# One PSUM pool of eight banks, rows transposed a tile ahead, and tiles dealt out in three runs, in a decoder layer with routed experts

## The chip, the cores and the metric

The kernel runs on one core of a Trainium2 chip. A core has five engines with instruction streams of their own: TensorE (matrix products and transposes, written to PSUM), VectorE, ScalarE, GpSimd (POOL in the profile) and SyncE (SP), which here only starts transfers. PSUM has eight banks of 128 partitions by 512 fp32 values. The metric is the device time of one execution in microseconds; of several executions the median is given.

## The reference

One decoder layer on 64 sequences of 128 positions with 256 features, all in fp32. Cut to what matters:

```
def attn(x):                                # a selective scan
    x_inner, z = split(layernorm(x) @ W_in)                 # 256 -> 2 x 512
    x_conv = silu(conv(x_inner, conv_w) + conv_b)           # 4 taps per channel
    Bmat, Cmat, delta = split(x_conv @ W_x)                 # 16, 16, 1
    h[t] = exp(delta[t] * A) * h[t-1] + delta[t] * Bmat[t] * x_conv[t]
    y = Cmat . h + x_conv * D_skip
    return (y * silu(z)) @ W_out + x

def xattn(q, c):                            # retention
    return ((xpos(q @ Wq) @ xpos(c @ Wk).T) * decay_mask) @ (c @ Wv)

def ffn(x):                                 # 8 experts, 2 per row, and a shared one
    shared = (silu(x @ shared_gate.T) * (x @ shared_up.T)) @ shared_down.T
    scores, indices = top_k(sigmoid(x @ router_w.T + routing_bias), 2)
    scores = scores / sum(scores)
    return shared + sum_k scores[k] * expert[indices[k]](x) # silu(gate) * up, then down; inner size 512

x = layernorm(x + attn(x)); x = layernorm(x + xattn(x, ctx)); x = layernorm(x + ffn(x))
```

## The kernel before

**Chains.** The 64 sequences go through in 16 groups (NG) of 4, 512 rows each. For each group `first_half` does layer norm, W_in, the convolution and the scan, which is written as products of decay matrices instead of a loop over positions. Its steps appear in the profile by their tiles: `w_in_s`, `xc`, `w_x_s`, `bcs`, `d` and `after_in` (sums of delta over positions), `cj` and `bj` (C and B with their decays, made on VectorE at L745), `mt` and `xd` (the decay matrix times the rows). `second_half` does W_out (`w_out_s`, `sz`), the retention, a layer norm, and then `route`: logits (`rw`, `logit`), the rank of each expert per row, the count of rows per expert so far (`sel`, `upto`, `pre`), and a scatter of each row to the place of its two experts in a DRAM buffer `xs`, by indirect DMAs on POOL. The comparisons that make ranks and the order mask `mk` (L968) are VectorE's, and the product `sel,upto` waits for them.

**The shared expert.** `shared` makes gate, up and down products for one group's 512 rows: per block of 128 inner features a gate and an up product, each filling a bank `psg`, `psu`; silu on ScalarE, the product with `up` on VectorE (`hc`, L1016), and at the end the down products. For nine groups this runs early, beside the next chains; for groups 7 to 13 (LATE) it runs at the end of the kernel.

**Routed tiles.** The rows in `xs` are worked off in 78 tiles of one expert each, in five batches (BATCHES: 9, 16, 16 and 16 tiles of 256 rows, after groups 4, 8, 12 and 16, and 21 of 128 rows at the end). `tile_list` makes each batch's table `what` on VectorE: tile number n (the constant `number`, an iota) is compared with the running sum `cum` of tiles per expert, which gives the tile's expert, its first row in `xs`, and a flag whether that expert differs from the one three tiles before. Three buffers of 1.5 MB (NW = 3) hold an expert's weights; tile i uses buffer i % 3, and its load is left out when the flag is zero. `fetch` starts both transfers on SP's queue: rows (L1142), then weights (L1148). `one_tile` calls `hidden` (the rows transposed to `rows_T`, copied out by ScalarE at L1166, then gate and up, silu at L1182, the product at L1183) and after it `down` of the tile before, whose rows are scaled by the routing weight (L1196) and scattered by POOL (L1197). Only when `down` has been called does `room` allow the load three tiles on. At the end `combine` gathers each row's two products, adds them, and does the last layer norm.

**PSUM.** Two pools share the eight banks: `pm` with five serves the chains, the transposes of tiles and their `down`; `gu` with three serves the shared expert and the gate and up products of tiles.

**What sets the order.** Each stage is a generator. `abreast` lets four of them run side by side (first halves, second halves, shared experts, tiles) and always continues the one that is least advanced in its due place, which `placed` gives it. The clock of this plan is `work`, to which every matmul and transpose adds an estimate; a `yield` with a number asks not to be continued for so long. `there` notes when a tile's rows and weights are to be expected. The order of emission then gives priorities, and the framework's scheduler lays out each engine's stream by priority, by readiness, and by the slots of the pools.

## Time and profile before

| | |
|---|---|
| three executions, median (lowest, highest) | 2053.07 us (2049.54, 2053.74) |
| profiled execution, its own time | 2046.0 us |
| its span, first to last instruction | 2044.3 us |
| mean granted TensorE clock in it | 0.984 |
| TensorE matmuls busy | 1894.9 us, 9252 instructions |
| VectorE, ScalarE, POOL busy | 988.5, 743.1, 462.0 us |
| read from HBM, written | 207.33 MB, 58.60 MB |
| SP's weight issues | 78 of 1536 KB |

A line of the timeline reads: start and length of a run of like instructions, engine, source line, operation, out<-in by the program's names, shape, how many; in square brackets the idle time before it and the instruction that ended it. Every fp32 product is recorded as two instructions. Line L543 is the helper that issues nearly all products, so that its groups are told apart by tile names. In the waits, a row names the engine and tile that waited, then the one that released it, then total, number and longest. A window's row has its two ends, its length, busy time and count of five engines, then the granted clock, the share of DMA time and GB/s.

### The profile page before, as it was taken

The page shows a single profiled execution, that of the slowest core. Times are in us where ns is not written, and L with a number is a line of the kernel's source. Part 1 is how long each engine was busy: PE and PEld are TensorE (multiplying, and loading weights), DVE is VectorE, ACT ScalarE, POOL GpSimd, SP SyncE. Part 2 cuts the span into 40 slices and gives each one's busy share as a digit, 9 for nine tenths or more (in the row PEclk, how much of TensorE's full clock was granted, in tenths as well). Part 3 has the DMA queues.
Part 4 walks back from the last instruction along what each step waited for, and adds up shares of the span by engine and source line. Part 5 has one row for each costly group of instructions (what it writes and reads, how often), then busy time and mean ns, then how long its engine had stood idle before and what let it go on. Part 6 is the DMA issues. An engine that isn't in the chain of part 4 may idle for free. (4 is left out here: it accounts for less than half of the span.)

```text
span 2044.3 us, 26096 instructions
## 1 busy us (share of the span) xinstructions
PE 1894.9 (93%) x9252; PEld 1396.5 (68%) x9252; DVE 988.5 (48%) x2398; ACT 743.1 (36%) x1239; POOL 462.0 (23%) x697
## 2 busy tenths in 40 slices
PE   4989998999999999999999999998998999999996
PEld 2655666686767676777777676767676888886553
DVE  3667676565555564555555555554431111012574
ACT  3355344344343534353434252534121222221332
POOL 3030221221212122323223121222123222221110
PEclk9899999999999999999999999999999999999998
DMA  4011121422313234333333442433224555862772
GB/s 146 26 54 44 53 64 39 165 90 75 124 44 109 59 135 150 111 126 124 129 121 100 150 140 80 134 116 116 104 80 166 183 184 195 305 218 97 256 268 84
DMA packets 100629, 253.60 MB, mean 124 GB/s; under 512 B 22824, under 2 KB 60328, under 8 KB 91528
## 3 DMA queue, kind: packets, MB, share of 16 engines
q1 hardware_dynamic: 77368, 196.56, 29.1%
q0 software_dynamic: 17616, 52.46, 7.4%
q10 hardware_dynamic: 5504, 2.81, 0.5%
q8 instruction: 75, 1.23, 0.2%
q14 instruction: 66, 0.54, 0.1%
HBM read 207.33 MB, written 58.60 MB: 130 GB/s over the span
## 5 line engine op out<-in xcount | busy, mean ns | idle before, releaser
L543 PE MATMUL gu<-rows_T,routed_w 128*128 128x256 f32 (+1 forms) x2496 | 511.2, 358 | 40.3 <-ACT rows_T L1166 14.8
L543 PEld LDWEIGHTS gu<-rows_T,routed_w 128*128 128x128 f32 x2496 | 421.5, 193 | 115.8 <-issue 34.1
L1183 DVE TENSOR_TENSOR hid<-hid,gu 128x512 f32<-128x512 f32 x135 | 92.3, 686 | 389.4 <-PE gu L543 370.5
L543 PE MATMUL pm<-routed_w,hid 128*128 128x256 f32 x1080 | 258.4, 383 | 9.9 <-DVE hid L1183 9.9
L543 PE MATMUL pm<-xnT,w_in_s 128*128 128x512 f32 x512 | 243.4, 600 | 3.2 <-ACT xnT L580 3.1
L543 PE MATMUL gu<-x2T,shared_w 128*128 128x512 f32 x512 | 230.5, 596 | 3.5 <-DVE hc L1016 2.6
L543 PEld LDWEIGHTS pm<-routed_w,hid 128*128 128x128 f32 x1080 | 198.6, 190 | 51.3 <-DVE hid L1183 14.7
L1197 POOL DMA_INDIRECT ys<-rows_out,to x135 | 138.4, 1026 | 325.5 <-ACT rows_out L1196 252.4
L562 POOL TENSOR_TENSOR rstd<-var,mhalf 128x4 f32<-128x4 f32 x64 | 68.2, 1066 | 508.7 <-DVE mv L558 282.7
L628 DVE SCALAR_TENSOR_TENSOR xc<-pm,cw,xc 128x508 f32<-128x508 f32 (+2 forms) x192 | 141.2, 740 | 77.9 <-ACT xc L623 74.3
L543 PEld LDWEIGHTS gu<-x2T,shared_w 128*128 128x128 f32 x512 | 94.6, 190 | 111.5 <-issue 99.6
L1182 ACT ACTIVATE hid<-gu 128x512 f32<-128x512 f32 x135 | 80.5, 596 | 237.6 <-PE gu L543 217.4
L543 PEld LDWEIGHTS pm<-xnT,w_in_s 128*128 128x128 f32 x512 | 95.6, 193 | 87.2 <-issue 74.1
L567 ACT ACTIVATE x<-x,shift,rstd 128x256 f32<-128x256 f32 x132 | 72.6, 591 | 183.1 <-DVE shift L564 183.1
L543 PE MATMUL pm<-w_out_s,sz 128*128 128x256 f32 x512 | 122.0, 391 | 9.3 <-DVE sz L784 8.3
L1196 ACT ACTIVATE rows_out<-pm,wt 128x256 f32<-128x256 f32 x135 | 57.7, 469 | 199.0 <-PE pm L543 148.5
L543 PE MATMUL gu<-shared_w,hc 128*128 128x256 f32 x512 | 116.7, 382 | 7.3 <-DVE hc L1016 7.3
L543 PEld LDWEIGHTS pm<-w_out_s,sz 128*128 128x128 f32 x512 | 98.5, 195 | 32.9 <-DVE sz L784 14.1
L543 PEld LDWEIGHTS gu<-shared_w,hc 128*128 128x128 f32 x512 | 95.4, 190 | 26.9 <-DVE hc L1016 11.1
L992 POOL DMA_INDIRECT xs<-x,index x64 | 66.9, 1045 | 138.3 <-issue 75.4
L781 DVE SCALAR_TENSOR_TENSOR xc<-xc,dsk,pm 128x512 f32<-128x512 f32 x64 | 47.2, 744 | 84.5 <-PE pm L543 56.3
L623 ACT ACTIVATE xc<-pm,cb,cw 128x512 f32<-128x512 f32 x64 | 49.7, 777 | 105.1 <-PE pm L543 105.1
(233 smaller groups left out, 2465.6 us busy)
## 6 DMA issues: line engine op xcount, KB each, us to landing
routed_w<-in_ffn_dram SPq DMA_DIRECT2D x78, 1536.0 KB
picked<-ys SPq DMA_DIRECT2D x16, 1024.0 KB
rows_in<-xs SPq DMA_DIRECT2D x57, 258.0 KB
cT<-in_ctxT_dram POOLq DMA_DIRECT2D x16, 512.0 KB
cq<-chunks SPq DMA_DIRECT2D x16, 512.0 KB
x_rows<-x SPq DMA_DIRECT2D x16, 512.0 KB
xt<-in_x_dram POOLq DMA_DIRECT2D x10, 512.0 KB
xt<-x_rows SPq DMA_DIRECT2D x10, 512.0 KB
```

The source lines that it names most:

```text
L543: nc.tensor.matmul(out, lhsT=lhsT, rhs=rhs, **how)
L562: nc.gpsimd.tensor_tensor(rstd, var, mhalf, ALU.pow)
L567: nc.scalar.activation(dst[:, b, :], src[:, b, :], AF.Identity, bias=shift[:, b : b + 1], scale=rstd[:, b : b + 1])
L623: nc.scalar.activation(xcf[:, c, :], ps, AF.Identity, bias=cb[:, c : c + 1], scale=cw[:, c, TAPS - 1 : TAPS],)
L628: nc.vector.scalar_tensor_tensor(xc[:, c, :, s:], ps3[:, :, : L - s], cw[:, c, TAPS - 1 - s : TAPS - s], xc[:, c, :, s:], ALU.mult, ALU.add,)
L781: nc.vector.scalar_tensor_tensor(y, xcf[:, c, :], dsk[:, c : c + 1], ps.rearrange("p b l -> p (b l)"), ALU.mult, ALU.add)
L992: s = nc.gpsimd.indirect_dma_start(out=xs, in_=rows[k][:, b, :], in_offset=None, out_offset=bass.IndirectOffsetOnAxis(ap=index[:, b, k : k ...
L1182: nc.scalar.activation(hc, psg, AF.Silu)
L1183: nc.vector.tensor_tensor(hc, hc, psu, ALU.mult)
L1196: nc.scalar.activation(y[:, j, :], ps[:, j, :], AF.Copy, scale=wt[:, j : j + 1])
L1197: s = nc.gpsimd.indirect_dma_start(out=ys, in_=y[:, j, :], in_offset=None, out_offset=bass.IndirectOffsetOnAxis(ap=to[:, j : j + 1], axis=0),)
```

## The change

There is one pool, `pm`, with eight banks; all its tiles share one tag, so any of them can take any bank. The transposes of a tile's rows, their copy to `rows_T`, and the small copies `to` and `wt` move to a function `rows_turned`. `hidden(i)` calls it for the next tile, between the two gate/up blocks of a 256-row tile or after the only one of a 128-row tile, if that tile's rows are due by `work`; otherwise the next `hidden` begins with it. And the constant `number` becomes a table for each size of batch, in which positions 0, 3, 6... hold the first third of the tile numbers, 1, 4, 7... the second and 2, 5, 8... the last, so that each weight buffer works through one run of the list.

```diff
-    pm = ctx.enter_context(tc.tile_pool(name="pm", bufs=5, space=bass.MemoryType.PSUM))
-    gu = ctx.enter_context(tc.tile_pool(name="gu", bufs=3, space=bass.MemoryType.PSUM))
+    pm = ctx.enter_context(tc.tile_pool(name="pm", bufs=8, space=bass.MemoryType.PSUM))
...
-            psg = gu.tile([P, T], F32, name="gu")
+            psg = pm.tile([P, T], F32, name="gu", tag="pm")
...
-            ge, number[:, 0:n].unsqueeze(2).to_broadcast([1, n, NE]),
+            ge, numbers[n].unsqueeze(2).to_broadcast([1, n, NE]),
...
-        nc.vector.scalar_tensor_tensor(row, number[:, 0:n], float(size), row, ALU.mult, ALU.add)
+        nc.vector.scalar_tensor_tensor(row, numbers[n], float(size), row, ALU.mult, ALU.add)
...
-    def hidden(i, t):
+    def rows_turned(i, t):
         _, size = shape(i)
-        w = weights[i % NW]
-        wg = w[:, 0:SZ].rearrange("p (k i) -> p k i", k=KD)
-        wu = w[:, SZ : 2 * SZ].rearrange("p (k i) -> p k i", k=KD)
         ps = pm.tile([P, KD, size], F32, name="pm")
...
-        yield 1.2
+        turned_rows.append((tT, to, wt))
+
+    turned_rows = []
+
+    def hidden(i):
+        _, size = shape(i)
+        w = weights[i % NW]
+        wg = w[:, 0:SZ].rearrange("p (k i) -> p k i", k=KD)
+        wu = w[:, SZ : 2 * SZ].rearrange("p (k i) -> p k i", k=KD)
+        if not turned_rows:
+            rows_turned(i, ahead.pop(0))
+            yield 1.2
+        tT, to, wt = turned_rows.pop()
         hid = []
         each = T // size
         for c0 in range(0, CF, each):
-            psg = gu.tile([P, each, size], F32, name="gu")
-            psu = gu.tile([P, each, size], F32, name="gu")
+            psg = pm.tile([P, each, size], F32, name="gu", tag="pm")
+            psu = pm.tile([P, each, size], F32, name="gu", tag="pm")
...
             hid += [hc[:, c, :] for c in range(each)]
+            if ahead and not turned_rows and there[i + 1] - 8.0 <= work[0]:
+                rows_turned(i + 1, ahead.pop(0))
         return hid, to, wt
...
-        made = yield from hidden(i, ahead.pop(0))
+        made = yield from hidden(i)
...
-    number = const.tile([1, MOST], F32, name="number")
-    nc.gpsimd.iota(number, pattern=[[1, MOST]], base=0, channel_multiplier=0,
-                   allow_small_or_imprecise_dtypes=True)
+    numbers = {}
+    for n in sorted({n for _, _, n, _ in BATCHES}):
+        t = const.tile([1, -(-n // NW), NW], F32, name=f"number{n}")
+        nc.gpsimd.iota(t, pattern=[[1, -(-n // NW)], [n // NW, NW]], base=0, channel_multiplier=0,
+                       allow_small_or_imprecise_dtypes=True)
+        for s in range(1, NW):
+            if n % NW:
+                nc.vector.tensor_scalar(t[:, :, s], t[:, :, s], float(min(s, n % NW)), None, ALU.add)
+        numbers[n] = t.rearrange("p k s -> p (k s)")[:, 0:n]
```

More of the change, by code (lines that the diff above doesn't have):

```diff
@@ L1009, in shared @@
         for c in range(CF):
-            psg = gu.tile([P, T], F32, name="gu")
+            psg = pm.tile([P, T], F32, name="gu", tag="pm")
             project(psg, wg, c * P, x2T)
-            psu = gu.tile([P, T], F32, name="gu")
+            psu = pm.tile([P, T], F32, name="gu", tag="pm")
             project(psu, wu, c * P, x2T)
@@ L1019, in shared @@
         for j in range(GB // 2):
-            ps = gu.tile([P, 2, D], F32, name="gu")
+            ps = pm.tile([P, 2, D], F32, name="gu", tag="pm")
             for i in range(2):
```

## The prediction

> **What bounds the kernel.** I read the page's busy shares first, then TensorE's waits, then its timeline around each wait. Columns of the waits: total us, times, longest.

> ```profile
> span 2044.3 us, 26096 instructions
> ...
> PE 1894.9 (93%) x9252; PEld 1396.5 (68%) x9252; DVE 988.5 (48%) x2398; ACT 743.1 (36%) x1239; POOL 462.0 (23%) x697
> ```

> TensorE is busy 1894.9 us of 2044.3 and no other engine passes 48%. So a microsecond counts only where it opens or closes a hole in TensorE's row, or slows its clock. The holes, about 135 us in all, are named by the waits:

> ```profile
> PE gu L543 <- ACT rows_T L1166: 14.8, 16, 3.2
> PE gu L543 <- DMA routed_w<-in_ffn_dram: 13.3, 6, 4.2
> PE gu L543 <- ACT hid L1182: 11.5, 7, 1.8
> ...
> PE pm L543 <- DVE mk L968: 10.4, 8, 4.0
> PE pm L543 <- DVE cj L745: 10.1, 5, 3.7
> ...
> PE pm L543 <- DVE hid L1183: 9.9, 17, 0.6
> ```

> Rows 1, 3 and 6 are what the change aims at: tiles that wait for their own turned rows, for a `gu` bank that ScalarE's silu has yet to empty, and for their own `hid`. Row 2 is all that 78 conditional loads cost today. The `mk` and `cj` rows are the chain's latency on VectorE (ranks, decay matrix), and matter because of what covers them:

> ```profile
> 187.29 4.56 PE L543 MATMUL gu<-x2T,shared_w 128*128 128x512 f32 x10
> 193.11 1.13 PE L543 MATMUL pm<-cj,bj 128*128 128x128 f32 x8 [1.25 <-DVE cj L745]
> ...
> 194.51 4.46 PE L543 MATMUL gu<-x2T,shared_w 128*128 128x512 f32 x10
> 199.53 0.38 PE L543 MATMUL pm<-sel,upto 128*128 128x32 f32 x2 [0.56 <-DVE mk L968]
> ...
> 201.45 3.59 PE L543 MATMUL pm<-mt,xd 128*128 128x128 f32 x30
> ```

> Two blocks of ten shared-expert matmuls, 9 us, lie inside the latencies of `cj` and `sel`, so holes of 1.25 and 0.56 are left. One group on, a single pair is left for the second place, and the hole is 3.97:

> ```profile
> 338.39 1.02 PE L543 MATMUL gu<-x2T,shared_w 128*128 128x512 f32 x2
> 343.38 0.61 PE L543 MATMUL pm<-sel,upto 128*128 128x32 f32 x2 [3.97 <-DVE mk L968]
> ...
> 347.11 4.67 PE L543 MATMUL pm<-mt,xd 128*128 128x128 f32 x30
> ```

> The same 30 matmuls took 3.59 and 4.67 us. The granted clock (the figure before the last two) says why:

> ```profile
> 343.60:347.00 3.40, 3.40 (x18) 3.40 (x18) 1.35 (x5) 2.53 (x5) 0.00 (x0) 0.50 0.00 0
> ...
> 1236.80:1240.20 3.40, 2.45 (x6) 1.99 (x7) 0.86 (x2) 0.00 (x0) 0.00 (x0) 0.50 0.00 0
> ```

> **The change, part by part.** The profiled run is 2046.0, its span 2044.3; the runs' median is 2053.07. I sum differences against 2046.0 and add them to the median.

> *(a) One pool of eight banks: where it frees.* With 5 and 3 banks a tile's second gate/up block needs a fourth `gu` bank and waits for a silu. In each of the six or seven groups between 795 and 1500 us the timeline shows the same holes: 0.76 (`rows_T`), 1.83 (`hid` L1182), 0.65 (`rows_T`), 0.44 (`x`). Three of the 16 `rows_T` waits lie elsewhere (0.74, 2.44, 0.1), so 11.6 of it goes here with part (b), the 11.5 of `hid` L1182 goes, and 2.3 of `x`. In the changed instruction order the router transpose (`logit`) stands without cover; by its neighbours (transpose out, copy, back) about 0.95, seven times. 11.6 + 11.5 + 2.3 - 6.6 = 18.8, **gain 19** (bounds 12 to 27). Between 370 and 750 us 3 of `rows_T` goes, and with the 2.44 hole its clock dip (10 us at 0.83, so 1.7): **gain 4.7**. From 1500 to 1600 one `hc` wait of 1.6 goes: **1.6**. In the last stretch (late shared experts) some bank waits go: **gain 3** (0 to 6).

> *(a) where it takes cover away.* The scheduler gives the slots of one pool out in program order. Before, shared-expert blocks had their own slots and were taken whenever the chain's next step wasn't ready, which is how 2, 5 and 5 matmul pairs got into each early group's latencies. In the changed order none stands between `rw` and `sel` in groups 1 to 4; they stand among w_out and w_in matmuls, where TensorE had nothing to wait for. The same work, hence no change of busy time, but the holes open: by the fourth group's bare `sel`, 3.97 plus the 0.6 to 1.0 it still had as cover, 4.6; at `cj` the fill was 4.6 and the hole 1.25, but two activation-table loads of 1.28 that the silu put into ScalarE's part of that chain leave too, so 2.2 to 2.8; `logit`, `d1` and `pre` 2.2 together. That is 9.5 a group where 2.2 were: 7.3 each for three groups, 4 for the fourth (half bare already), less the 2.2 that group 1 waits for `xnT` today: **loss 23** (10 to 30). At the eighth group, 720 to 745 us, 12 tile matmuls and 8 shared ones leave the same place, and `cj` and `sel` follow bare: **loss 8** (3 to 10).

> *The clock.* After the 3.97 hole TensorE ran at 0.50 for about 6.8 us: the transposes of `xc` and `mt,xd` took 2.8 to 3.0 us longer than the same ones at 199 to 205. Three more holes of 4.6, each behind one of 2.5, are as deep: 3 x 3.0 = 9.0, the fourth 0.7 more, the eighth group 2.0 (a dip of 1.7 stands nearby already). **Loss 11.7.** [...] holes of 1.39 and 1.28 within 4 us were followed by 0.50 at 1236.8[...]. Against it, the same pair at 1340 and 3.15 at 1416 brought nothing. I take the row of the like hole, 3.0[...].

> *(b) Rows turned a tile ahead.* The 2 or 4 transposes, the copy to `rows_T` (L1166) and POOL's copies `to` and `wt` move from the head of a tile into the one before; none is added. Their rows must land one tile earlier; they are loaded up to three tiles ahead, so I cost it at nothing; if SP is late, TensorE stands behind the transposes for up to a load, about 2 us. POOL's two small copies now precede the scatter of the tile before; POOL is at 23%. `down` of a tile now follows the gate/up of the next, so the late 128-row tiles lose this hole:

> ```profile
> 1779.08 3.73 PE L543 MATMUL gu<-rows_T,routed_w 128*128 128x128 f32 x32
> 1782.65 0.38 PE L547 MATMUL pm<-ident,rows_in 128*128 128x128 f32 x2
> 1783.66 1.99 PE L543 MATMUL pm<-routed_w,hid 128*128 128x256 f32 x8 [0.63 <-DVE hid L1183]
> 1785.49 3.73 PE L543 MATMUL gu<-rows_T,routed_w 128*128 128x128 f32 x32
> ```

> 17 x 0.63 and a bank wait of 1.04 at 1760: **gain 11.7**. But the buffer comes free one tile later. From the end of `down` to the gate/up that needs the next load there are then 3.57 + 0.3 + 1.83 = 5.7 us. An undisturbed load takes 6.35 to 6.45 from issue to its last packet at 1805 to 1824, and 0.2 passes before the issue: 0.85 late. Behind it wait that gate/up and everything on TensorE. Six or seven executed loads: **loss 6** (3 to 15). [...] The trace's own loads decide. With 256-row tiles the window is 10.8, and a load is hidden.

> *(c) Tiles dealt in three runs.* With the reference's routing the load flag is set in 69 of 78 tiles before and in 39 after; 30 x 1.57 MB = 47 MB less of 207. All but six loads are hidden, so this alone is worth little: at 1549, 1582 and 1597 (4.24, 2.33, 2.86) the first three loads of a batch remain, behind SP's zero-fill transfers: nothing either way (0 to -3). In the late tiles 12 of 21 are left out, which is why only six or seven stall above. Two more iotas on POOL stand ahead of the first groups' half-width transposes: **loss 0.5**.

> **Sum.** Gains 19 + 4.7 + 1.6 + 3 + 11.7 = 40.0; losses 23 + 8 + 11.7 + 6 + 0.5 = 49.2. Net +9.2: span 2053.5, run 2055.2, median 2053.07 + 9.2 = **2062**.

> **Rivals.**
> 1. *Faster, 2037.* The early latencies shrink by more than I think when the shared silu leaves ScalarE and its product VectorE: each table load is 1.28, each `hc` product 0.69. If the chain ends 4 us sooner in each of four groups and the eighth, [...]the clock holds: losses 10 + 3 + 4 + 6 + 0.5 = 23.5 against 40, 2053 - 16.5. It decides once early holes, eighth group and clock together cost under 33. For it: the tables in the chain. Against: VectorE runs from 193 to 200 with no hole wider than 0.1, and the `hc` products are 0.7 of it before `sel`.
> 2. *Slower, 2083.* The holes come as forecast, and the late loads follow one another: stall 2 instead of 0.85 (+8), the gain between 795 and 1500 only 12 (+7), early holes at their upper end (+6). For it: 0.89 DMA share in that stretch before. Against: fewer loads share the engines now.
> 3. *No change, 2054.* All moved holes come back in kind[...]. The loads left out don't show, hidden before as after.

> **Numbers.** Forecast 0.52 (own range 2054 to 2073), faster 0.23, slower by more 0.13, no change 0.12. Repeats of this kernel differ by up to 0.2%, 4.1 us, so that is about what can be told from no change. The forecast's lower end gives part of its chance to "same": faster 0.24, same 0.16, slower 0.60. Range: 2038 takes in all but the deepest of the faster case, 2080 most of the slower.

> **What will show it.** Right: in groups 1 to 3, `sel` behind `mk` with 4 us or more and a slice of clock at 0.5 behind each; `rows_T` and `hid` L1182 gone from the waits, `hid` L1183 too; `routed_w` waits of about 0.9 in the late tiles; about 160 MB read. Wrong: `sel` holes under 2 in groups 1 to 3, a new cover there, or late stalls of 2 us or none.

## The result

The changed kernel takes 2062.14 us (median of six runs, 2058.88 to 2067.45) against 2053.4 for the kernel before on the same chip (2048.97 to 2056.0): 1.0049 times, 95% interval 1.0031 to 1.0066. It is slower by about 8.7 us; 9 were forecast. Lines of the changed kernel's page, and the line on transfers of the kernel before:

```profile
span 2057.2 us, 26112 instructions
...
PE 1896.3 (92%) x9252; PEld 1412.8 (69%) x9252; DVE 993.6 (48%) x2400; ACT 742.9 (36%) x1236; POOL 460.9 (22%) x699
...
DMA packets 96307, 206.39 MB, mean 100 GB/s; under 512 B 22344, under 2 KB 59848, under 8 KB 91048
```

```profile
DMA packets 100629, 253.60 MB, mean 124 GB/s; under 512 B 22824, under 2 KB 60328, under 8 KB 91528
```

TensorE's busy time rose by 1.4 us only, the span of the profiled execution by 12.9. That is more than the 8.7 of the medians: the profiled execution of before took 2046.0 us, less than any of the six just named, so a few us of the comparisons by trace below may not be the change's. The transfers fell from 253.60 to 206.39 MB, the 47 MB that were worked out. (The page's HBM line still says 207.33 MB read: it doesn't tell the loads that are left out.) The mean granted clock fell from 0.984 to 0.967. The largest of TensorE's waits, changed kernel (total us, times, longest):

```profile
PE pm L542 <- DVE cj L744: 27.6, 6, 6.3
PE pm L542 <- DVE mk L967: 26.2, 11, 4.6
PE gu L542 <- DMA routed_w<-in_ffn_dram: 21.0, 8, 5.0
```

The rows of before that the change aimed at (`rows_T` 14.8, `hid` L1182 11.5, own `hid` 9.9) are gone. In their place `cj` went from 10.1 to 27.6, `mk` from 10.4 to 26.2, the weights from 13.3 to 21.0. Group 3 in the timeline:

```profile
275.55 1.08 PE L542 MATMUL pm<-middle,dlb 128*32 128x128 f32 x32
282.72 2.05 PE L542 MATMUL pm<-cj,bj 128*128 128x128 f32 x8 [6.09 <-DVE cj L744]
...
288.78 0.60 PE L542 MATMUL pm<-sel,upto 128*128 128x32 f32 x2 [3.16 <-DVE mk L967]
...
292.11 4.90 PE L542 MATMUL pm<-mt,xd 128*128 128x128 f32 x32
```

There is no shared-expert block between these steps any more. And the clock in the same place, by windows (length, busy time of PE, PEld, DVE, ACT and POOL; last three columns: granted clock, DMA share, GB/s):

```profile
279.40:282.80 3.40, 0.08 (x1) 0.11 (x1) 1.93 (x5) 0.00 (x0) 0.00 (x0) 0.72 0.03 9
282.80:286.20 3.40, 2.82 (x12) 2.42 (x12) 3.40 (x6) 0.54 (x1) 0.00 (x0) 0.50 0.00 0
```

The product `sel,upto` starts once per group, so its sixteen starts cut both traces into like stretches ("5th sel" is its start in the fifth group). Difference to the kernel before, us, with the forecast's sum for the same stretch:

| stretch | forecast | measured | worked out from the starts |
|---|---|---|---|
| start to 5th sel | +33.2 | +35.3 | 463.96 - 428.64 |
| 5th to 7th | -4.7 | -3.3 | 192.26 - 195.52 |
| 7th to 8th | +10.0 | +7.4 | 101.56 - 94.12 |
| 8th to 16th | -19.0 | -25.3 | 777.23 - 802.55 |
| 16th to end | -10.3 | -1.3 | 522.2 - 523.5 |
| span | +9.2 | +12.9 | 2057.2 - 2044.3 |

So the early loss was sized well, the middle gained more than I said, and the stretch with the late tiles gained nearly nothing. That the sum came out so close is in part luck, since these two misses cancel.

### The profile page after: what moved, and what is told of

The parts are those of the page before. It is cut to its first block, busy times and chain, and to the rows that moved or that the text cites. A ratio compares the mean times of both kernels' runs of the same rounds, so it can differ in the third digit from the quotient of the medians.

```text
span 2057.2 us, 26112 instructions
## 1 busy us (share of the span) xinstructions
PE 1896.3 (92%) x9252; PEld 1412.8 (69%) x9252; DVE 993.6 (48%) x2400; ACT 742.9 (36%) x1236; POOL 460.9 (22%) x699
## 2 busy tenths in 40 slices
DMA packets 96307, 206.39 MB, mean 100 GB/s; under 512 B 22344, under 2 KB 59848, under 8 KB 91048
## 3 DMA queue, kind: packets, MB, share of 16 engines
HBM read 207.33 MB, written 58.60 MB: 129 GB/s over the span
## 4 chain that ended last, share of the span: by engine, by line
PE 67%; DVE 9%; DMA 8%; issue 8%; ACT 3%; POOL 2%; SPq 0%; another core or an unknown queue 0%; DVEq 0%; POOLq 0%; ACTq 0%
PE pm L542 36%; PE gu L542 27%; PE pm L546 4%; DMA cq<-chunks 3%; DMA routed_w<-in_ffn_dram 2%; DMA x_rows<-x 1%; POOL rstd L561 1%; DVE gq L756 1%; DVE eq L752 1%; DVE eq L751 1%; DVE st L556 1%; DMA picked<-ys 1%; POOL ys L1207 1%; DVE xc L780 1%; ACT L692 0%
## 5 line engine op out<-in xcount | busy, mean ns | idle before, releaser
L542 PE MATMUL gu<-rows_T,routed_w 128*128 128x256 f32 (+1 forms) x2496 | 504.1, 355 | 21.1 <-DMA routed_w<-in_ffn_dram 21.0
L542 PEld LDWEIGHTS gu<-shared_w,hc 128*128 128x128 f32 x512 | 96.8, 192 | 30.5 <-DVE hc L1015 12.1
L1014 ACT ACTIVATE hc<-gu 128x512 f32<-128x512 f32 x64 | 37.8, 591 | 132.0 <-PE gu L542 120.0
```

Source lines behind the costliest of these rows:

```text
L542: nc.tensor.matmul(out, lhsT=lhsT, rhs=rhs, **how)
L1014: nc.scalar.activation(hc, psg, AF.Silu)
```

## The experiments

All ratios are to the kernel before, measured on the same chip in the same set; the sets ran on different chips, so kernels of two sets are compared by their ratios only. The ratios are those on record for a whole set; the quotient of two medians given below can differ from them by up to 0.2%. The stretches of all kernels, as in the table above (one profiled execution each, us against the one profile of before, so small differences mean little; the 5th to 7th sel is left out):

| kernel | to 5th | 7th to 8th | 8th to 16th | 16th to end | ratio (95% interval) |
|---|---|---|---|---|---|
| changed kernel | +35.3 | +7.4 | -25.3 | -1.3 | 1.0049 (1.0031 to 1.0066) |
| pool_only | +39.9 | +1.1 | +3.2 | +23.7 | 1.0391 (1.0357 to 1.0425) |
| deal_only | +0.7 | 0.0 | -4.0 | -3.8 | 0.9953 (0.9933 to 0.9972) |
| ahead_only | +1.7 | +8.0 | -3.8 | +4.9 | 1.0042 (1.0026 to 1.0058) |
| two_pools | -0.4 | +7.3 | -17.4 | -3.3 | 0.9923 (0.9900 to 0.9946) |
| slot_late | +32.5 | +4.5 | -34.4 | +6.7 | 0.9996 (0.9977 to 1.0016) |
| warm | +37.5 | +8.7 | -27.7 | -1.4 | 1.0025 (1.0014 to 1.0036) |
| no_deal | +38.6 | +8.1 | -13.5 | +12.1 | 1.0208 (1.0174 to 1.0242) |
| after_halves | +37.3 | +7.3 | -36.2 | -21.5 | 0.9897 (0.9876 to 0.9919) |
| two_slot | +8.5 | +4.8 | -28.0 | -1.0 | 0.9893 (0.9871 to 0.9916) |
| halves | +12.4 | +4.6 | -29.0 | -24.0 | 0.9770 (0.9744 to 0.9797) |
| halves_plain | +6.4 | +7.3 | -28.6 | -24.2 | 0.9762 (0.9741 to 0.9782) |
| halves62 | +14.7 | +7.0 | -36.8 | -15.1 | 0.9826 (0.9806 to 0.9847) |

### Which part does what: the parts one by one

**The pool alone.** The kernel before with one pool:

```diff
-    pm = ctx.enter_context(tc.tile_pool(name="pm", bufs=5, space=bass.MemoryType.PSUM))
-    gu = ctx.enter_context(tc.tile_pool(name="gu", bufs=3, space=bass.MemoryType.PSUM))
+    pm = ctx.enter_context(tc.tile_pool(name="pm", bufs=8, space=bass.MemoryType.PSUM))
...
-            psg = gu.tile([P, T], F32, name="gu")
+            psg = pm.tile([P, T], F32, name="gu", tag="pm")
```

> The kernel before with one pool of eight banks, nothing else. Theory (cover lost to the single pool): the shared expert's blocks leave the latencies of cj and sel in groups 1 to 4, so there are sel holes of 3 to 4.6 us with the clock at 0.5 behind them, about +35 between the first and the fifth sel as in the changed kernel; the eighth group keeps its cover in this instruction order, so nothing there; the bank waits (hid L1182, part of rows_T) go between 800 and 1500, about -15. Net +15 to +22, some 2070 us. Rival (the loss belongs to the rows turned ahead, not to the pool): early groups as before, net -15, some 2038 us.

Measured 2120.07 us, 1.0391, 76 us more than before (2044.13), where 15 to 22 were expected. The early loss is there in full and the eighth group keeps its cover, as expected. But the gain between 800 and 1500 isn't there, and the late tiles lose 24 us. A wait of TensorE in it:

```profile
PE gu L542 <- ACT rows_T L1165: 67.6, 52, 3.5
```

The waits on `rows_T` went from 14.8 to 67.6. In the kernel before, the transposes of the next tile had a pool beside that of gate and up, and among the late tiles of its trace they stand ahead of the `down` of the tile before (1782.65 and 1783.66, shown in the prediction). In pool_only they stand behind it (`down` at 1853.45, transposes at 1855.18), and gate and up wait for them at once: on the average each of the 52 waits is 1.3 us. That the scheduler can't draw them forward because one pool gives out its slots in program order fits this order, but was not tested by itself. The pool alone is the loss; turning the rows ahead in the program is what makes it bearable.

**The dealing alone.**

```diff
-    number = const.tile([1, MOST], F32, name="number")
...
+    numbers = {}
```

> The kernel before with the tiles dealt in three runs, nothing else. Theory: all but six loads were hidden, so the 47 MB that are left out are worth nothing in the stretch beside the chains and at most the 1.0 us wait at 1760: 0 to -3, about 2052 us, with the HBM transfers at 206 instead of 254 MB. Rival (less traffic quickens the other transfers, on which chains wait): -8 or more.

Measured 2034.78 us, 0.9953: the rival's. I had costed this at nothing, and the interval ends at 0.9972. TensorE's waits on weights fell by 4.0 us only (13.3 to 9.3). VectorE's waits name another transfer. First the kernel before, then the dealing alone:

```profile
DVE eq L752 <- DMA cq<-chunks: 14.4, 8, 3.3
```

```profile
DVE eq L752 <- DMA cq<-chunks: 9.3, 5, 3.5
```

`cq` is 512 KB that the scan's chain reads back on the same queue. A wait of VectorE doesn't count by itself, only by what TensorE then waits for: TensorE's waits on `rows_T` fell by 3.9 us as well (14.8 to 10.9), those on `mk` by 1.4, and all its waits together from 133.2 to 126.6, which are the 6.6 us by which the span fell (2044.3 to 2037.7). So the gain is spread over waits for several things. That `cq` and the rows come sooner because 30 loads are left out is argued, not shown.

**The rows ahead alone, and with the dealing.** The first keeps two pools and the old numbers; the second is the changed kernel with this line undone:

```diff
-    pm = ctx.enter_context(tc.tile_pool(name="pm", bufs=8, space=bass.MemoryType.PSUM))
+    pm = ctx.enter_context(tc.tile_pool(name="pm", bufs=5, space=bass.MemoryType.PSUM))
+    gu = ctx.enter_context(tc.tile_pool(name="gu", bufs=3, space=bass.MemoryType.PSUM))
```

> The kernel before with the rows transposed a tile ahead, two pools and the old dealing. Theory: the waits on rows_T and on the own hid go (-12 in the late tiles, some -8 between 800 and 1500), but each late tile's load now starts with 5.7 us left where it needs 6.6: about 15 executed loads in the late batch stall 0.9 to 1.8 each, +14 to +25; the eighth group loses its cover, +7. Net 0 to +15, some 2060 us. Rival (loads start in time as SP's queue is free): net -12, 2041 us.

> The changed kernel with the two pools of five and three banks put back, so the rows a tile ahead and the dealing alone. Theory: the early groups keep the cover of the shared expert and cost what they did before (-35 against the changed kernel), the eighth group stays bare as its order is the same, the bank waits between 800 and 1500 come back in part. Against the kernel before: +7 at the eighth group, -8 to -15 in 800 to 1500, -1 to -5 in the late tiles. Net -5 to -12, some 2045 us. Rival (the early loss comes from the tiles' dealing or the rows ahead): 2060 us or more.

Measured 1.0042, as the theory had it, and 0.9923 (2027.82 us), about 16 us by the medians, more than the 5 to 12 expected. With two pools the early groups cost what they did before. So the three parts are not a sum: rows ahead +0.4%, dealing -0.5%, both together -0.8%, and the pool on top of both +1.3%, where alone it is +3.9%. The eighth group's loss comes with the rows ahead (+8.0 and +7.3) and not with the pool (+1.1).

The parts show something else in the tiles from 750 to 1500 us. In ahead_only, which keeps the three `gu` banks, TensorE waits for no silu there any more, and for `rows_T` 5.0 us only. So the rows turned ahead removed both waits, and the larger pool wasn't needed for that. But the same kernel then waits for the product `sel`:

```profile
PE pm L543 <- DVE sel L949: 14.1, 4, 3.8
```

With the waits on `mk` that is 26.1 us there, against 4.4 in the kernel before and 12.7 in two_pools, which has the dealing besides; VectorE's waits on `cq` there are 20.7 in ahead_only and 8.3 in two_pools. With the rows ahead the ranks are left with less cover, and with the dealing half of that wait is gone.

**The dealing undone in the changed kernel.**

> The changed kernel with the tile numbers in the old order, so 69 loads instead of 39. Theory (dealing pays only where a load isn't hidden, which since the rows are turned ahead is the late batch): 15 executed late loads instead of 6 or 7, 1.6 us each, +13 to +16, some 1.012 of the kernel before. Rival (dealing is worth its 9 us of the kernel before through less traffic, at whatever place): the same size but spread over the stretch beside the chains, the late tiles within 4 us.

Measured 1.0208, 1.6% over the changed kernel. The late stretch lost 13.4 us (12.1 + 1.3), as the theory had it, and the stretch from the 8th to the 16th sel 11.8, as the rival had it. Each of the two theories had left out the other's stretch, so each was too small, with 13 to 16 us against 33 by the ratios. The same wait of VectorE, changed kernel first, then with the old numbers:

```profile
DVE eq L751 <- DMA cq<-chunks: 9.1, 6, 3.2
```

```profile
DVE eq L751 <- DMA cq<-chunks: 23.0, 9, 4.1
```

### What makes the early holes so long

**The copy that waits for a store.** The forecast for the `cj` holes was 2.2 to 2.8 us; they are 4.2, 6.1 and 4.7 in groups 2 to 4 and 6.3 in the eighth. VectorE's timeline in the changed kernel shows what stands ahead of `cj`:

```profile
280.87 0.17 DVE L964 COPY x<-slot 128x4 f32<-128x4 f32 x1 [3.52 <-DMA x_rows<-x]
...
281.88 0.69 DVE L744 TENSOR_TENSOR cj<-cj,eb 128x512 f32<-128x512 f32 x1
```

A copy of four numbers per partition into a row buffer waits until the 512 KB store of an earlier group's rows, which reads that buffer, has landed. In the changed kernel these waits are 14.3 us, in four places. The kernel before has them too, one of 2.96 us at 190.57, under the shared expert's matmuls:

```profile
DVE x L965 <- DMA x_rows<-x: 7.8, 3, 3.0
```

The experiment makes the copy depend on the ranks, so that it can only come later:

```diff
-        nc.vector.tensor_copy(rows[0][:, :, D], slot[:, g * GB : (g + 1) * GB])
+        nc.vector.scalar_tensor_tensor(
+            rows[0][:, :, D], rank[:, :, 0], 0.0, slot[:, g * GB : (g + 1) * GB], ALU.mult, ALU.add
+        )
```

> The changed kernel, with VectorE's copy of the slot numbers (L964) made to depend on the ranks, so that it can no longer stand ahead of bj and cj and wait there for the store x_rows. Theory (the cj holes of 4.2, 6.1, 4.7 and 6.3 in groups 2 to 4 and 8 are this copy waiting for a transfer): they fall to 2.0 to 2.8, so 12 to 14 us less between the first and the eighth sel, and with less clock loss some 15 in all: 1.0049 becomes about 0.998 of the kernel before. Rival (the chain itself is as long, the copy only fills the time): under 3 us, 1.004.

Measured 2050.65 us, 0.9996: 0.5% less than the changed kernel. Group 3 now:

```profile
281.87 1.98 PE L542 MATMUL pm<-cj,bj 128*128 128x128 f32 x8 [2.54 <-DVE cj L744]
...
288.16 0.38 PE L542 MATMUL pm<-sel,upto 128*128 128x32 f32 x2 [3.46 <-DVE x L964]
```

The `cj` hole is 2.54 in groups 2 to 4, the value of the forecast. Between the first and the eighth sel it is 9.7 us less, where 12 to 14 were expected: the waits on `cj` there fell from 21.3 to 11.2, the eighth keeps 3.5, and the waits for `sel` grew by 1.6. Behind the 16th sel it is 8.0 us longer than the changed kernel and from the 8th to the 16th 9.1 shorter, which the late copy doesn't explain.

**The clock.** 32 transposes of the identity, read by nobody, fill each of the two holes in the five bare groups:

```diff
+        if st["bare"]:
+            idle = pm.tile([P, T], F32, name="idle", tag="pm")
+            for r in range(32):
+                nc.tensor.transpose(idle[:, r % 4 * P : (r % 4 + 1) * P], ident, ident)
```

> The changed kernel, with 32 transposes of the identity, read by nobody, put on TensorE ahead of cj,bj and ahead of sel in the five bare groups; 3.5 us each at full clock, less than the holes. Theory (the clock falls in the holes, and the work behind them pays): the granted clock stays at 1.0 from 100 to 390 and from 740 to 770, mt,xd takes 3.6 again, 3 to 4 us less in each of five groups: 15 to 18 us in all, about 0.997 of the kernel before. Rival (the holes alone cost, work after them is not slowed): no gain, or a loss of what the transposes stick out, 1.005 or more.

Measured 1.0025: 0.24% less than the changed kernel, a third of what was expected and hardly to be told, since the two intervals overlap; the stretches of its trace show none of it. Group 3:

```profile
278.10 3.71 PE L743 MATMUL idle<-ident 128*128 128x128 f32 x32
285.24 1.13 PE L542 MATMUL pm<-cj,bj 128*128 128x128 f32 x8 [3.43 <-DVE cj L748]
...
286.64 5.32 PE L964 MATMUL idle<-ident 128*128 128x128 f32 x32
291.80 0.31 PE L542 MATMUL pm<-sel,upto 128*128 128x32 f32 x2
```

The filling did not reach to the end of the first hole (3.43 us of it stayed), and the clock still fell (0.68 in 285.40 to 288.80, 0.82 in 288.80 to 292.20). The second filling ran slowly (5.32 instead of 3.71) and ended after VectorE was ready. As a measure of the clock's price this run failed. The price can be read without it: from `sel` to the first product of `w_out_s` it took 5.35 in groups 2 and 3 of the kernel before (199.53 to 204.88, 271.80 to 277.15), 7.18 and 8.07 in the changed kernel (205.66 to 212.84, 288.78 to 296.85), and 6.57 and 6.10 in this run. So 1.8 and 2.7 behind each hole, of which the filling won back 0.6 and 2.0.

### The late tiles

In the changed kernel six of the nine late loads that are executed are waited for, 11.2 us together. TensorE, then SP's queue, in one such place:

```profile
1785.84 1.89 PE L542 MATMUL pm<-routed_w,hid 128*128 128x256 f32 x8
...
1794.83 3.81 PE L542 MATMUL gu<-rows_T,routed_w 128*128 128x128 f32 x32 [1.57 <-DMA routed_w<-in_ffn_dram]
```

```profile
1787.76 0.33 SPq L1147 DMA_DIRECT2D routed_w<-in_ffn_dram  x1
```

The load starts when the `down` that frees its buffer has ended, at 1787.73, and is used 7.07 us later. Four of the six loads are used 7.07 to 7.35 us after their issue, and one, issued 5.5 us behind another, after 8.39. The sixth wait is the longest, and has another cause:

```profile
1769.50 5.25 PE L542 MATMUL gu<-rows_T,routed_w 128*128 128x128 f32 x32 [3.61 <-DMA routed_w<-in_ffn_dram]
```

```profile
SPq L1139 <- POOL rows_in L1138: 6.9, 1, 6.9
```

Its buffer was free at 1758.9, but its load went out at 1763.20 only and took 6.30 us to be used. SP's queue stood for 6.9 us waiting for a copy of the table's entry by POOL. That copy stood in POOL's queue behind the copy `to`, which the change moved a tile forward, and which had waited 5.36 us for a scatter to end. ahead_only has the same wait (3.73 us).

To see whether the buffer or the queue sets the start of the loads, gate/up and down weights got buffers and transfers of their own, so that the first 1 MB waits for gate and up of three tiles before only:

```diff
+        for part, cols in zip(weights[i % NW], (slice(0, 2 * SZ), slice(2 * SZ, 3 * SZ))):
+            nc.sync.dma_start(
+                out=part, in_=ffn[bass.ds(e, 1), :, cols].rearrange("o p n -> (o p) n"),
+                cond=(new != 0), bounds_check="skip_entire_dma",
+            )
```

> The changed kernel with each expert's weights in two buffers and two transfers, nothing else. Theory (the late loads are late because the buffer comes free a tile later): the six routed_w waits between 1760 and 1856 (11.3 us) and the clock dip behind the longest (1.7) go, and of the 9.9 us at 1563 and 1596 some part, because the first halves are free earlier: -13 to -20, some 0.996 of the kernel before. Rival (SP's queue or the engines' bandwidth, not the buffer, sets the loads' end): under 4 us, 1.003.

Measured 2029.92 us, 0.9897: 1.5% less than the changed kernel, about 31 us, more than expected. The late stretch gave 20.2; from the 8th to the 16th sel it is 10.8 shorter too, which I had not expected and whose cause isn't settled (TensorE waited less there for `mk`, 7.1 us instead of 12.2, and for `xnT`, 2.9 instead of 6.5). The waits on weights are down from 21.0 to one:

```profile
PE gu L542 <- DMA routed_w<-in_ffn_dram: 4.1, 1, 4.1
```

So for five of the six waits the buffer was the limit, not the queue; at the sixth SP waited for POOL, which it does in this kernel for 0.3 us only. The first pieces are issued 7.8 to 8.1 us before they are used, in the changed kernel about 5.5 before they are wanted. That would be enough for the 7.1 to 7.4 of an undivided load too. What the smaller piece gives besides the earlier start was not separated.

### A version that beats both

Four kernels put the good parts together: two pools, rows ahead, dealing. With the late copy (two_slot), with the late copy and halves (halves), with halves alone (halves_plain), and halves with two banks for the shared expert and six for all else (halves62).

> The kernel with two pools, rows ahead and dealing (0.9923 of the kernel before), with the copy of the slot numbers made to depend on the ranks. Theory: bare cj waits of group 8 (6.4 us there) and the 1.2 of the covered groups shrink, 5 to 9 us, about 0.989. Rival: nothing, as the cover lies over the same wait, 0.992.

> The same as the one with two pools and the late copy, with each expert's weights in two buffers and two transfers: gate and up (1 MB) and down (0.5 MB). Theory (late tiles stall because the load waits for down of three tiles before): the gate and up part is free one down and one turn of rows earlier, so its 1 MB starts 5 us sooner, and the routed_w waits of 0.9 to 1.5 in the late tiles go, 5 to 8 us less than without it: about 0.986. Rival (SP's queue starts the first half no sooner because it stands behind the second half of the tile before): no change.

> Two pools, rows ahead, dealing and the weights in halves, with the copy of the slot numbers where it was. Theory: the late copy lost some 9 us in the early groups and won 7 at the eighth and behind it, so within 0.3% of 0.977 either way. Rival (the late copy was the gain): 0.981 or more.

> The same with two banks for the shared expert alone and six for the chains and all of a tile. Theory: the shared expert's own slots are what keeps the cover in the early groups, so they stay as before; tiles find a bank more often, which is worth the few waits on banks that are left, and the late shared experts lose one of three banks: 0.972 to 0.98. Rival (two banks are too few for gate and up in turn with down): hc waits of 2 us per block, 0.985 or more.

Measured 0.9893 (0.9871 to 0.9916), 0.9770 (0.9744 to 0.9797), 0.9762 (0.9741 to 0.9782) and 0.9826 (0.9806 to 0.9847). Where the early groups are covered, the late copy makes no difference that could be told: the intervals of two_slot and two_pools overlap, and so do those of halves and halves_plain. The halves are worth 1.2 to 1.6%. Six banks and two are worse than five and three, so my theory of it fell: to the fifth sel halves62 lost 14.7 us against the kernel before, 8.3 more than halves_plain, with waits on `xnT` of 13.7 us there instead of 2.7. It gained 9 less behind the 16th sel and 8 more from the 8th to the 16th. halves_plain, 2001.78 us against 2051.21 before, is the fastest kernel of the study by its median.

## Why the prediction was right, and where it was not

**The time was right, the stretches less so.** Two misses cancel: the middle gained 6.3 us more than forecast, the stretch behind the 16th sel 9.0 less.

**(a) where it takes cover away: right, and it is the pool.** pool_only and two_pools show it from both sides (+39.9 and -0.4 to the fifth sel). The early holes named in the sum add to 23.7, not 23, which changes nothing. The two holes together were 7.3 to 9.3 in groups 2 to 4 instead of 6.8 to 7.4, and the split was wrong: `cj` 4.2 to 6.1 instead of 2.2 to 2.8, because VectorE stood at L964 for a store (slot_late), a wait that the trace of before shows too and the prediction had left out; `sel` 3.2 instead of 4.6, because the products between the two holes ran at a granted clock of 0.50 (`cj,bj` and `xc` 3.1 us in group 3 instead of 1.7) and filled part of the second.

**The eighth group: right in size (7.4 against 10 with the clock), wrong in cause.** I put it to the pool; it comes with the rows ahead.

**The clock: right in kind.** In group 3 the clock read 0.50 from 280.90, within the hole of 6.1, to 294.55, past 2.8 us of work and the hole of 3.2, and it fell in all five bare groups. In group 3 it fell 4.3 us into the hole of 6.1; in group 1 at 110.2, behind no hole over 1.56 us; in groups 2, 4 and 8 at 0.2, 1.7 and 3.1 us into the hole. So the length of a hole alone did not decide it: in the kernel before the clock stayed at 1.00 around the hole of 3.15 at 1416. The last section has the numbers. The price behind a hole was 1.8 and 2.7, not 3.0, and the slow work between the holes cost nothing, since VectorE was the later one.

**(a) where it frees: larger than forecast (25.3 against 19), and wrongly attributed.** The waits on `rows_T` and `hid` L1182 went, but the rows ahead take them away with three `gu` banks too (ahead_only): no fourth bank was needed. And two_pools already gains 17.4 of the 25.3 between the 8th and the 16th sel without the pool, and the pool alone has none of it. Nor does it belong to the rows ahead alone (-3.8) or to the dealing alone (-4.0). It takes both, since the rows ahead open waits on `sel` that the dealing halves.

**(b) the late tiles: the mechanism right, the price too low.** The wait on the own `hid` went. The term that was too small is "0.85 late": four of the six loads were used 7.1 to 7.4 us after their issue, not 6.35 to 6.45 plus 0.2. The last packet had been taken for the end, and the load issued 5.5 us behind another was used after 8.39. The longest wait, 3.61, came from POOL's small copies, which were costed at nothing. The waits between 1760 and 1856 are 11.2 us instead of 6, with 1.4 of lost clock behind the longest (5.25 us for products that take 3.81 elsewhere, at 0.50 from 1769.11 to 1772.52).

**(a) the last stretch, forecast gain 3: not there.** The `hc` waits behind 1870 us are 9.0 us instead of 8.3. From 1500 to 1600 the `hc` wait of 1.6 went and one of 3.9 on a tile's rows came.

**(c) "nothing either way": wrong.** Alone it is -0.5%, and in the changed kernel its absence costs 1.6%. The misreading is "Row 2 is all that 78 conditional loads cost today": TensorE's wait on the loads fell by 4.0 us of the 6.6 that the dealing alone took from the span, and the rest is in waits that name other things.

**The rivals.** The slower one named late stalls of 2 instead of 0.85; five of 1.1 to 1.9 and one of 3.6 were seen, but the middle gained more, not less. The faster one, that the chain is shorter without the shared silu, didn't come. No change lies outside the interval of the difference (6.4 to 13.5 us). Of the signs, the `sel` holes of 4 us or more came in group 1 only (4.4; then 3.2 and 3.2).

## What to carry to other kernels

Where a scheduler fills the latencies of a chain with other work, a separate pool for that work is what lets it be drawn forward (to the fifth sel -0.4 us in two_pools, +39.9 in pool_only); more banks in one pool can cost more than the waits on banks that they remove (3.9% in pool_only). Before a wait in an engine's queue is costed by the arithmetic of its chain, look for small instructions in that queue that wait for a transfer (14.3 us of VectorE's at L964 in the changed kernel). And where a buffer's release sets a load's start, splitting the buffer by its first and its last reader can give more time than another order of the work (here 1.2 to 1.6%, the late copy 0.5%).

## What the runs showed of the hardware that was not expected

**The clock.** In group 3 the granted clock fell within the first of two holes of 6.1 and 3.2 us, with 2.8 us of work between them, and stayed at 0.50 for 13.65 us. In the run with the fillings it fell behind a hole of 3.43 us although TensorE had been busy for 3.7 us just before. In each of the two traces of before and after, all its changes lie on one raster of 3.41 us; in the kernel before for example at 342.54, 540.51 and 619.01, which are 58 and 23 steps apart, in the changed kernel at 110.23, 127.30, 195.57, 202.39, 280.90 and 294.55, which are 5, 20, 2, 23 and 4 steps apart. Cut by this raster, the windows before its falls at 110.23 and 195.57 read so, the first with the one behind it:

```profile
106.82:110.23 3.41, 0.60 (x17) 0.20 (x9) 1.04 (x7) 3.35 (x7) 0.00 (x0) 1.00 0.27 81
110.23:113.64 3.41, 2.97 (x35) 2.01 (x35) 2.80 (x8) 1.43 (x2) 1.66 (x2) 0.50 0.52 137
192.16:195.57 3.41, 1.91 (x43) 1.25 (x35) 2.99 (x6) 1.84 (x4) 1.26 (x1) 1.00 0.72 197
```

**The loads.** Undisturbed loads of 1.5 MB, issued at 1798.52 to 1817.76 in the trace of before, ended their last packet 6.35 to 6.44 us after the issue; in that of the changed kernel the products that waited for one started 7.07 to 7.35 us after it in four places (6.30 and 8.39 in the other two). In the changed kernel, between the last packet of a load and the start of the products that waited for it, there lay 0.66 to 0.81 us in five places and 0.47 in one.
